# A network of attention, MLP and convolution on one core: LayerNorm multiplications placed elsewhere, two more taps for ScalarE, other banks and pace for the last image

## The chip, the cores and the metric

One core of a Trainium2 chip runs the whole program as one launch. The metric is device time in microseconds (us), the median of three runs. Engines are named as in the profile: PE is TensorE (matmuls), DVE is VectorE, ACT is ScalarE, POOL is GpSimd, SP is SyncE.

## The reference, cut to what matters

Eight images of 384 channels by 32 x 32 pixels, all in 32-bit floats. Each goes through a transformer block and then through a convolution block:

```python
# layer 0, tokens n = 1024 pixels, 8 heads of 48
xn = layernorm(x, g1, beta1);  q, k, v = xn @ w_qkv.T + b_qkv
x1 = softmax(q @ k.T * SCALE) @ v @ w_proj.T + b_proj + x
y  = x1 + gelu(layernorm(x1, g2, beta2) @ w_fc1.T + b_fc1) @ w_fc2.T + b_fc2   # hidden 1536
# layer 1
z = depthwise_conv_7x7(y) + dw_b
z = gelu(layernorm(z, ln_w, ln_b) @ w1 + b1)                                   # hidden 1536
gx = sqrt(sum over pixels of z*z);  nx = gx / (mean(gx) + eps)
out = y + (grn_gamma * (z * nx) + grn_beta + z) @ w2 + b2
```

The LayerNorms are called LN1 (ahead of q, k, v), LN2 (ahead of w_fc1) and LN3 (ahead of w1) below.

## The kernel before, in words

Channels lie on the 128 partitions, three tiles of them (CT = 3); pixels lie along the free axis, 1024 of them in two halves of 512. The images go through one after the other (main, L1611 on): the attention and the MLP of image b come first, then, inside the same pass of the loop, the second half of the convolution block of image b-1 (w1, GRN, w2), so that VectorE can convolve image b-1 while TensorE does the attention and the MLP of image b.

**Matmuls.** Attention is plain. fc1 is plain too, in halves of 512 tokens: gelu_half takes one ps_o bank, three matmuls and a Gelu on ScalarE (L457). fc2, w1, w2 and q/k use a fast scheme on 3 x 2 blocks with 15 products instead of 18, which needs sums of blocks. by_thirds (L919) does fc2 and w2: it forms sums of blocks of the hidden tensor, named f, h, e, g, by VectorE (L953) while the products run, and each product waits for its sum. tiles_by_thirds (L407) does w1 and q/k: here the block sums of the input are made ahead by make_thirds (L404) and VectorE adds up the outputs (L432) from single banks.

**PSUM.** Two pools: ps_s has two tiles of 128 x 1024 (attention's scores, every other product of fc2), ps_o has four tiles of 128 x 512 (everything else, the sums of the LayerNorms among them).

**Order.** The order of the instructions on each engine is that of the program, and the program is written out by a planner, Flow (L136). Flow.now is a clock that advances by U = 0.857 us with every full matmul that is written. A piece of side work is a Python generator (a chain); what it yields is the time until its next step is due, and a step is written once the clock has passed its due time. A paced chain counts from its due times, so that it catches up. finish(chain) writes all that is left of it at once.

**LayerNorm.** layernorm (L486) adds up the three tiles of channels on VectorE (L501, L503), has TensorE sum over the partitions with a matrix of ones (token_sums, L460), subtracts the mean (VectorE, L510), squares (ScalarE, L517), adds (L524), sums again, takes ln and exp on ScalarE (L534, L535) and multiplies (VectorE, L538). With fold, a GpSimd DMA first adds one half of the partitions onto the other (L475) and the ones matmul is half as large (L481); without, it is 128 x 128 (L467). abreast (L545) runs the two halves of an image as one chain, with all yields multiplied by factor (1.4).

- LN2 of the first half runs beside the end of attention (L810), spaced out and folded by "columns"; that of the second half runs beside fc1 of the first half (mlp, L893 on).
- LN3 of image b-1 (conv_norm, L1667) starts when LN2 of image b is through, after end_soon (L1700), which finishes the convolution's chains and then waits. It runs beside fc1's second half and fc2.
- LN1 of image b+1 (norm_of_next, L1704) runs beside the same stretch, with sums in places, four tiles of the pool tag "res". Its multiplications (L1757) come after a yield of 4.0, and are finished ahead of grn_up (the w1 matmuls).
- before_fc2 (L1760) finishes what is left of the convolution and spawns make_thirds for w1, after LN3.

**Convolution.** Of the 49 taps, convolution (L1072) writes 42 as VectorE instructions (L1098; the first L1096). The other seven (HELPED, L68) belong to help_convolution (L1103): for each tap and half of the image, ScalarE multiplies the window into a "res" tile (L1119), and a GpSimd DMA adds that onto the accumulator (L1120). It goes 2.7 us at a step, holds while `quiet` is set (the averages of attention, w2), and keeps VectorE off a tile of channels while it is at it (taken). For image 0, start_conv (L1661) is called behind its MLP; its convolution lies beside image 1's attention. The last image's convolution is written in two parts of its rows (last_convolution, L1783), each with its own pace; its LN3 goes in three parts of the pixels (LAST: 416, 288 and 320), and last_up (L1242) multiplies a part by w1 when its LN3 is finished.

**Image 0's preparations.** The sums of weight blocks and the products of weights with bias vectors are formed at the start, beside image 0, by the chains folds, prepare and sums_for_tiles. In shift_through_w2 (L1499), VectorE multiplies a third of w2 by grn_beta and adds it up (L1509 to L1511), and after a yield of 4.0 a matmul with ones takes the column sums (L273).

Of the kernel before, what the change touches and what calls it, by code (L numbers as in the profile page):

```python
# [46 lines left out]
F32 = mybir.dt.float32  # L47
# [4 lines left out]
P = 128  # L52
B, C, H, W = 8, 384, 32, 32
N = H * W
CT = C // P
# [120 lines left out]
def block_kernel(  # L176
# [280 lines left out]
        nc.scalar.activation(dst, src, function, **kw)  # L457
        table[0] = None

    def token_sums(t, name, fold, wait):  # L460

        width = t.shape[-1]
        if fold is None:
            total = o_tile(name)[:, :width]
            nc.tensor.matmul(out=total, lhsT=ones, rhs=t, start=True, stop=True)  # L467
            flow.pe(U * width / NH)
            return [(total, slice(0, width))]
        rows = [slice(0, 64), slice(64, P)]  # L470
        parts = [(fold, slice(0, width))]
        if fold == "columns":
            parts = [(j, slice(j * width // 2, (j + 1) * width // 2)) for j in range(2)]
        for j, cols in parts:
            nc.gpsimd.dma_start(out=t[rows[j], cols], in_=t[rows[1 - j], cols], accum_op=ALU.add)  # L475
        yield wait
        totals = []
        for j, cols in parts:
            total = o_tile(f"{name}_{j}")[:, : cols.stop - cols.start]
            for i in rows:  # L480
                nc.tensor.matmul(out=total[i, :], lhsT=ones[rows[j], :64], rhs=t[rows[j], cols], start=True, stop=True)  # L481
            flow.pe(U * width / NH / 2)
            totals.append((total, cols))
        return totals

    def layernorm(src, dst, h, eps, g, name, switch, spare=None, spaced=False, slow=1.0, fold=None, wait=3.4, gentle=False):  # L486

        cols = h if isinstance(h, slice) else half(h)
        if isinstance(h, slice):
            h = h.start
        width = cols.stop - cols.start
        if spare:
            a, *squares = (t[:, :width] for t in spare())
            rstd = a
        else:
            a = one.tile([P, NH], F32, tag="ln_a", name=f"{name}_a{h}")[:, :width]
        nc.vector.tensor_tensor(a, src[:, 0, cols], src[:, 1, cols], ALU.add)  # L500
        if gentle:  # L501
            yield 1.2
        nc.vector.tensor_tensor(a, a, src[:, 2, cols], ALU.add)  # L503
        yield 2.6 * slow
        totals = yield from token_sums(a, f"{name}_sum{h}", fold, wait)
        yield 0.8
        for ct in range(CT):
            for total, part in totals:
                to, of = dst[:, ct, cols][:, part], src[:, ct, cols][:, part]
                nc.vector.scalar_tensor_tensor(to, total, -1.0 / C, of, ALU.mult, ALU.add)  # L510
            if gentle:
                yield 1.2
        yield 0.8 * slow
        if not spare:
            squares = [three.tile([P, NH], F32, tag="ln_sq", name=f"{name}_sq{h}_{ct}")[:, :width] for ct in range(CT)]
        for ct in range(CT):
            nc.scalar.activation(squares[ct], dst[:, ct, cols], AF.Square)  # L517
            if spaced:
                yield 1.7
        yield 0.8 if spaced else 1.8 * slow  # L520
        nc.vector.tensor_tensor(squares[0], squares[0], squares[1], ALU.add)
        if gentle:
            yield 1.2
        nc.vector.tensor_tensor(squares[0], squares[0], squares[2], ALU.add)  # L524
        yield 1.8 * slow
        totals = yield from token_sums(squares[0], f"{name}_var{h}", fold, wait)
        yield 0.8

        if not spare:
            rstd = one.tile([P, NH], F32, tag="ln_rstd", name=f"{name}_rstd{h}")[:, :width]  # L530
        if switch:
            ln_table()
        for var, part in totals:
            nc.scalar.activation(rstd[:, part], var, AF.Ln, bias=eps, scale=1.0 / C)  # L534
        nc.scalar.activation(rstd, rstd, AF.Exp, scale=-0.5)  # L535
        yield (2.6 if switch else 1.2) * slow
        for ct in range(CT):
            nc.vector.scalar_tensor_tensor(dst[:, ct, cols], dst[:, ct, cols], col(g, ct), rstd, ALU.mult, ALU.mult)  # L538
            if gentle and ct < CT - 1:
                yield 1.2  # L540
# [1 line left out]
    def averages():  # L542
        return [attn[:, i, :] for i in range(4)]

    def abreast(*args, places=averages, fold=True, wait=3.4, gentle=False, factor=1.4):  # L545

        how = dict(wait=wait, gentle=gentle)
        chains = [
            layernorm(*args[:2], h, *args[2:], spare=places if h else None, fold=h if fold else None, **how)
            for h in range(2)  # L550
        ]
        while chains:
            waits = []
            for chain in list(chains):
                wait = next(chain, None)
                if wait is None:
                    chains.remove(chain)
                else:
                    waits.append(wait)
            if waits:  # L560
                yield factor * max(waits)
# [182 lines left out]
    def attention(b, xt, qT, kT, last_tile, ready, first, next_image):  # L744
# [44 lines left out]
        for n in range(len(steps) + 2):  # L789
            if n == 2:  # L790
                last_tile()
            if n < len(steps):
                if steps[n][0] == 0 and steps[n][2] == 0:
                    ready(steps[n][1])
                ps[n] = scores(*steps[n])
            if n >= 2:
                product(*steps[n - 2], ps.pop(n - 2))
            if n - 2 in (len(steps) // 2 - 9, len(steps) - 9):
                quiet.append("averages")
            if n - 2 == len(steps) // 2 + 6:  # L800
                for chain in first:
                    flow.finish(chain)
                xn = one.tile([P, CT, N], F32, tag="xn", bufs=2, name=f"xn2_{b}")
                next_image(b)
                for m in (NP - 1, *range(CT)):
                    flow.finish(chains[0, m])
                proj(b, xt, 0)
                quiet.clear()
                slow = 1.2 if b in (1, B - 1) else 1.0
                ln = layernorm(xt, xn, 0, eps0, "g2", f"ln2_{b}", False, spaced=True, slow=slow, fold="columns", wait=4.5)  # L810
                ln = flow.spawn(ln)

        def rest():
# [255 lines left out]
        rows, cols = inside(dy, dx, y0, y1)  # L1069
        return 120 + (rows.stop - rows.start) * (cols.stop - cols.start)  # L1070

    def convolution(acc, us, first=(), y0=0, y1=H, ready=tuple(range(CT)), taken=None):  # L1072

        done = [0] * CT
        ct, n = None, 0
        taps = KS * KS - (HELPED if taken is not None else 0)

        shares = [size(*divmod(i, KS), y0, y1) for i in TAPS[:taps]]  # L1080
        shares = [taps * s / sum(shares) for s in shares]
# [18 lines left out]
            n += 1  # L1100
            yield share * next((early for m, early in first if n <= m), us)

    def help_convolution(acc, us, taken):  # L1103

        yield 8.0
        for ct in reversed(range(CT)):
            taken[ct] = float("inf")
            for i in TAPS[KS * KS - HELPED :]:
                dy, dx = divmod(i, KS)
                for h in range(2):  # L1110
                    if quiet:
# [294 lines left out]
    def prepare(weights, aside):  # L1406
# [92 lines left out]
        def shift_through_w2():  # L1499
            for r in range(CT):  # L1500
# [8 lines left out]
                nc.vector.tensor_tensor(t[:, 0], t[:, 0], t[:, 1], ALU.add)  # L1509
                for k in range(1, h):  # L1510
                    nc.vector.tensor_tensor(t[:, 0, 0, :], t[:, 0, 0, :], t[:, 0, k, :], ALU.add)  # L1511
                yield 4.0
                ps = ps_s.tile([P, N], F32, tag="s", name=f"b2_{r}")
                column_sums(ps, 0, t[:, 0, 0, :])
                nc.vector.tensor_tensor(b2[:, r : r + 1], ps[:, :1], col("b2", r), ALU.add)
# [95 lines left out]
    def main():  # L1611
# [49 lines left out]
        def start_conv(b, us, *first):  # L1661
            acc = state["acc"] = one.tile([P, CT, N], F32, tag="acc", name=f"acc_{b}")
            taken = {}
            state["conv"] = flow.spawn(convolution(acc, us, first, taken=taken), paced=True)
            state["help"] = flow.spawn(help_convolution(acc, 2.7, taken), paced=True)

        def conv_norm(b, ln):  # L1667

# [3 lines left out]
                state["norm1"] = flow.spawn(after(ln, norm))  # L1672
            else:
                acc = state["acc"]
                how = dict(wait=5.0) if b < B - 1 else dict(wait=3.4, factor=2.4)
                norm = abreast(acc, acc, eps1, "lnw", f"ln3_{b - 1}", True, **how)
                if b < B - 1:
                    state["norm1"] = flow.spawn(after(ln, norm_of_next(b, 22.0 if b > 1 else 34.0)))
# [25 lines left out]
        def norm_of_next(b, us):  # L1704
# [8 lines left out]

            def total(t, h, kind):
                if kind == "sum":
                    ps = ps_s.tile([P, N], F32, tag="s", name=f"{name}_sum{h}")[:, :NH]
                else:
                    ps = o_tile(f"{name}_var{h}")
                for i in rows:
# [30 lines left out]
            for h, a, _ in pairs:  # L1750
                nc.scalar.activation(a, sums[h], AF.Ln, bias=eps0, scale=1.0 / C)
                nc.scalar.activation(a, a, AF.Exp, scale=-0.5)
            yield 4.0
            for h, a, _ in pairs:
                for ct in range(CT):
                    part = xn[:, ct, half(h)]
# [26 lines left out]
        def last_convolution(h, ct, ln=None):  # L1783
# [5 lines left out]
            ready[h].append(ct)  # L1789
            if ct == 0:  # L1790
                rows = (LAST[0].stop // W, H) if h else (0, LAST[0].stop // W)
                conv = convolution(last[0], 0.86 if h else 0.66, (), *rows, ready[h])
                state["conv"] = flow.spawn(after(state["conv"], conv), paced=True)
                if h == 0:
                    state["norm_a"] = flow.spawn(after(state["conv"], last_norm(LAST[0], 2.6)))

        for b in range(B):
# [29 lines left out]
            flow.finish(state["norm3"])  # L1827
            if b < B - 1:
                flow.finish(state["w1"])
                flow.finish(state["norm1"])  # L1830
                y, gx = grn_up(b - 1, weights, b - 1)
                start_conv(b, 1.6 if b == B - 2 else 1.65, (23, 2.4), (24, 9.0), (25, 26.0))
                scale = flow.spawn(grn_scale(b - 1, gx, weights, b - 1, y))
# [175 lines left out]
```

## Time and profile before

| what | us |
|---|---|
| median of three runs | 3280.41 (3280.2 to 3284.95) |
| profiled execution | 3279.71 |
| its span (1.8 lies around it) | 3277.9 |
| PE busy | 3239.4 (99%) |
| DVE busy | 2432.0 (74%) |
| ACT busy | 1662.0 (51%) |
| POOL busy | 480.3 (15%) |
| mean granted TensorE clock | 0.995 of full speed |

How to read it: the page gives busy times of each engine in one execution; a group of instructions is told by line, engine, operation and tile, out<-in. The waits of an engine list what its idle time ended with: "PE fc_p L445 <- ACT fc_n L943" is a matmul of line 445 into the tile fc_p that started when ScalarE's instruction of line 943 was done. A timeline gives start, duration, instruction and, in brackets, the idle time ahead of it with its releaser. A matmul of 128 x 512 has two records that overlap; start to start a full one takes 0.858 us. PEclk is the clock granted to TensorE. Where the work of the changed places lies, by the timeline: w2's shift at 100 to 160, LN2 of image 0 at 165 to 240, LN2 of image 1's second half until 531, fc2 and w1 of image 1 at 585 to 640, fc2 of image 3 at 1775 to 1800, LN3 of image 6 about 2950, and the last image's second part about 3150.

### The profile page before, as it was taken

The numbers are of one execution on the slowest core, as the hardware profiler recorded it, in microseconds if no ns is written. First come the engines' busy times: TensorE is split into PE (matmuls) and PEld (weight loads), VectorE is DVE, ScalarE is ACT, GpSimd is POOL, SyncE is SP. The second block draws the span as 40 slices with busy tenths as digits, with TensorE's granted clock in tenths as the row PEclk, the third lists the DMA queues.
The fourth block names the chain that finished last, engine by engine and source line by source line (L and its number), as shares of the span: only waits on it lengthen the run. The fifth ranks groups of instructions, "written<-read, shape, count | busy, mean of one in ns | idle before, by whom it ended". The sixth has DMA issues, their size and how long they took to land. (4 is left out here: it accounts for less than half of the span.)

```text
span 3277.9 us, 38879 instructions
## 1 busy us (share of the span) xinstructions
PE 3239.4 (99%) x14216; PEld 1399.7 (43%) x14216; DVE 2432.0 (74%) x3318; ACT 1662.0 (51%) x2317; POOL 480.3 (15%) x567
## 2 busy tenths in 40 slices
PE   9999999999999999999999999999999999999999
PEld 5344444343344433344344443444434443344455
DVE  4644788777877878768788687876888778879850
ACT  3442663356643475444753647537474365623631
POOL 2121211112110121101211012110221112200000
PEclk9999999999999999999999999999999999999999
DMA  6635742647335573446635375353843638433231
GB/s 213 221 100 121 165 87 57 156 108 172 82 65 154 120 161 75 87 138 153 139 64 115 110 189 100 63 128 103 204 91 67 157 91 189 73 79 85 68 91 54
DMA packets 202706, 384.82 MB, mean 117 GB/s; under 512 B 41104, under 2 KB 47120, under 8 KB 202128
## 3 DMA queue, kind: packets, MB, share of 16 engines
q0 software_dynamic: 81472, 166.50, 26.9%
q1 hardware_dynamic: 120752, 215.09, 21.5%
q8 instruction: 114, 1.87, 0.2%
q10 hardware_dynamic: 288, 0.71, 0.1%
q14 instruction: 80, 0.66, 0.1%
HBM read 199.61 MB, written 38.14 MB: 73 GB/s over the span
## 5 line engine op out<-in xcount | busy, mean ns | idle before, releaser
L1098 DVE SCALAR_TENSOR_TENSOR acc<-pad,vec,acc 128x870 f32<-128x870 f32 (+8 forms) x861 | 963.6, 1156 | 6.9 <-DMA acc<-tap 1.7
L764 ACT ACTIVATE p<-s 128x1024 f32<-128x1024 f32 x512 | 524.1, 1024 | 274.4 <-PE s L755 266.7
L755 PE MATMUL s<-qk 48*64 48x512 f32 x4096 | 549.5, 594 | 0.5 <-ACT qk L601 0.5
L775 PE MATMUL o<-p,v 64*64 64x512 f32 x4096 | 547.5, 593 | 0.0
L378 PE MATMUL fc<-xn,fc 128*128 128x512 f32 x1152 | 505.9, 596 | 2.1 <-DVE acc L510 2.1
L1120 POOL DMA_DIRECT2D acc<-tap x294 | 253.6, 872 | 1437.5 <-ACT tap L1119 704.2
L378 PEld LDWEIGHTS fc<-xn,fc 128*128 128x128 f32 x1152 | 217.7, 190 | 286.0 <-issue 275.6
L445 PE MATMUL fc_p<-hid,fc 128*128 128x512 f32 x728 | 319.7, 594 | 5.2 <-DVE hid L953 2.4
L775 PEld LDWEIGHTS o<-p,v 64*64 64x64 f32 x4096 | 168.1, 133 | 277.4 <-issue 269.0
L755 PEld LDWEIGHTS s<-qk 48*64 48x64 f32 x4096 | 163.4, 133 | 278.8 <-issue 223.8
L457 ACT ACTIVATE hid<-fc,bfc_f 128x512 f32<-128x512 f32 x192 | 129.9, 684 | 297.3 <-PE fc L378 297.2
L445 PE MATMUL o_p<-y,w 128*128 128x512 f32 x624 | 270.9, 592 | 0.0
L1119 ACT ACTIVATE tap<-pad,vec 128x512 f32<-128x512 f32 x294 | 215.8, 734 | 1.8 <-DMA acc<-tap 1.8
L445 PEld LDWEIGHTS fc_p<-hid,fc 128*128 128x128 f32 x728 | 137.0, 190 | 184.5 <-issue 169.4
L445 PEld LDWEIGHTS o_p<-y,w 128*128 128x128 f32 x624 | 118.0, 190 | 148.7 <-issue 134.9
L1098 DVE SCALAR_TENSOR_TENSOR acc_last<-pad,vec,acc_last 128x377 f32<-128x377 f32 (+24 forms) x288 | 177.3, 691 | 0.6
L887 ACT COPY pad<-x 128x512 f32<-128x512 f32 x48 | 30.2, 634 | 266.2 <-DVE x L953 209.2
L716 DVE TENSOR_TENSOR attn<-o,attn 128x512 f32<-128x512 f32 x64 | 44.1, 690 | 125.2 <-ACT attn L714 125.2
L697 PE MATMUL proj<-attn,wproj_sb 128*128 128x512 f32 x288 | 127.5, 596 | 0.7 <-DVE attn L742 0.7
L675 PE MATMUL v<-wv_sb,xn 128*128 128x384 f32 x384 | 126.8, 487 | 0.0
L432 DVE TENSOR_TENSOR y<-h_n,y 128x512 f32<-128x512 f32 x72 | 49.8, 692 | 74.6 <-PE h_n L416 72.2
L675 PEld LDWEIGHTS v<-wv_sb,xn 128*128 128x128 f32 x384 | 72.5, 190 | 50.1 <-issue 3.3
(376 smaller groups left out, 4068.3 us busy)
## 6 DMA issues: line engine op xcount, KB each, us to landing
acc<-tap POOLq DMA_DIRECT2D x294, 256.0 KB, 3.5
fc<-s_fc SPq DMA_DIRECT2D x91, 256.0 KB, 3.0
w<-s_w SPq DMA_DIRECT2D x72, 320.0 KB, 3.1
hid<-hid POOLq DMA_DIRECT2D x42, 512.0 KB, 7.1
fc<-in_wfc SPq DMA_DIRECT2D x54, 384.0 KB, 4.0
w<-s_w SPq DMA_DIRECT2D x78, 256.0 KB, 2.7
y<-y POOLq DMA_DIRECT2D x36, 512.0 KB, 6.8
w_A<-in_w SPq DMA_DIRECT2D x36, 384.0 KB, 3.2
```

What stands on the lines that cost most here:

```text
L378: nc.tensor.matmul(out=ps, lhsT=lhsT(k), rhs=rhs(k)[:, half(h)], start=(k == 0), stop=(k == nk - 1))
L432: nc.vector.tensor_tensor(c[dst], banks(name), c[other], ALU.add)
L445: nc.tensor.matmul(out=bank, lhsT=lhsT, rhs=rhs, start=k == 0, stop=k == len(pairs) - 1)
L457: nc.scalar.activation(dst, src, function, **kw)
L675: nc.tensor.matmul(out=ps[:, :C], lhsT=xn[:, k, t * P : (t + 1) * P], rhs=wv_sb[:, k, :], start=(k == 0), stop=(k == CT - 1),)
L697: nc.tensor.matmul(out=ps, lhsT=wproj_sb[:, m, ct * P : (ct + 1) * P], rhs=attn[:, m, :], start=(m == 0), stop=(m == CT - 1),)
L755: nc.tensor.matmul(out=s[64 * i : 64 * i + 64, j, :], lhsT=kT[64 * j : 64 * j + HD, m, k0 : k0 + 64], rhs=qT[64 * j : 64 * j + HD, m, half ...
L764: nc.scalar.activation(p, s, AF.Exp)
L775: nc.tensor.matmul(out=outs[i][64 * j : 64 * j + 64, :], lhsT=v[keys, t, at : at + 64], rhs=p[keys, j, :], start=(t == 0), stop=(t == KT - 1),
L1098: nc.vector.scalar_tensor_tensor(dst, window, tap, dst, ALU.mult, ALU.add)
L1119: nc.scalar.mul(t.rearrange("p (h w) -> p h w", w=W), window, tap)
L1120: nc.gpsimd.dma_start(out=acc[:, ct, half(h)], in_=t, accum_op=ALU.add)
```

## The change

1. s_tile gives a ps_s tile; token_sums, layernorm and abreast take `bank`, from which the sums' tile comes. For the last pass (LN3 of image 6), bank is s_tile.
2. layernorm takes `late`, added to the yield ahead of its multiplications. LN3 of the other images has late=3.5 (4.9 after the factor).
3. norm_of_next yields 50.0 instead of 4.0 ahead of its multiplications, and is no longer finished ahead of grn_up; it is finished by next_values, behind grn_up.
4. LN2 of image 0's first half isn't folded.
5. ScalarE has nine taps instead of seven for image 0 (convolution and help_convolution take `helped`).
6. shift_through_w2 yields 8.0 instead of 4.0 ahead of its matmul (three times).
7. The second part of the last convolution has a pace of 0.76 us instead of 0.86 per tap.

```diff
+    def s_tile(name):
+        return ps_s.tile([P, N], F32, tag="s", name=name)
+
-    def token_sums(t, name, fold, wait):
+    def token_sums(t, name, fold, wait, bank):
...
-            total = o_tile(f"{name}_{j}")[:, : cols.stop - cols.start]
+            total = bank(f"{name}_{j}")[:, : cols.stop - cols.start]
...
-    def layernorm(src, dst, h, eps, g, name, switch, spare=None, spaced=False, slow=1.0, fold=None, wait=3.4, gentle=False):
+    def layernorm(src, dst, h, eps, g, name, switch, spare=None, spaced=False, slow=1.0, fold=None, wait=3.4, gentle=False, bank=o_tile, late=0):
...
-        yield (2.6 if switch else 1.2) * slow
+        yield (2.6 if switch else 1.2) * slow + late
...
-                ln = layernorm(xt, xn, 0, eps0, "g2", f"ln2_{b}", False, spaced=True, slow=slow, fold="columns", wait=4.5)
+                fold = "columns" if b else None
+                ln = layernorm(xt, xn, 0, eps0, "g2", f"ln2_{b}", False, spaced=True, slow=slow, fold=fold, wait=4.5)
...
-        taps = KS * KS - (HELPED if taken is not None else 0)
+        taps = KS * KS - helped
...
-            for i in TAPS[KS * KS - HELPED :]:
+            for i in TAPS[KS * KS - helped :]:
...
-                yield 4.0
+                yield 8.0
                 ps = ps_s.tile([P, N], F32, tag="s", name=f"b2_{r}")
...
-            state["conv"] = flow.spawn(convolution(acc, us, first, taken=taken), paced=True)
-            state["help"] = flow.spawn(help_convolution(acc, 2.7, taken), paced=True)
+            helped = HELPED if b else HELPED + 2
+            state["conv"] = flow.spawn(convolution(acc, us, first, taken=taken, helped=helped), paced=True)
+            state["help"] = flow.spawn(help_convolution(acc, 2.7, taken, helped), paced=True)
...
-                how = dict(wait=5.0) if b < B - 1 else dict(wait=3.4, factor=2.4)
+                how = dict(wait=5.0, late=3.5) if b < B - 1 else dict(factor=2.4, bank=s_tile)
...
-            yield 4.0
+            yield 50.0
             for h, a, _ in pairs:
                 for ct in range(CT):
                     part = xn[:, ct, half(h)]
...
-                conv = convolution(last[0], 0.86 if h else 0.66, (), *rows, ready[h])
+                conv = convolution(last[0], 0.76 if h else 0.66, (), *rows, ready[h])
...
                 flow.finish(state["w1"])
-                flow.finish(state["norm1"])
                 y, gx = grn_up(b - 1, weights, b - 1)
```

## The prediction

> **What bounds the kernel now.** I read the busy times first, then TensorE's waits over the run, then the timeline and the windows around each wait that the change touches.
>
> ```profile
> span 3277.9 us, 38879 instructions
> PE 3239.4 (99%) x14216; PEld 1399.7 (43%) x14216; DVE 2432.0 (74%) x3318; ACT 1662.0 (51%) x2317; POOL 480.3 (15%) x567
> ```
>
> TensorE is busy for 99% of the span and idle for 38.5 us. No matmul of weight goes away, so all that can be won is in these waits and in slow matmuls behind them:
>
> ```profile
> PE fc_p L445 <- ACT fc_n L943: 5.6, 5, 1.1
> PE b L273 <- DVE w_gbeta L1511: 3.0, 1, 3.0
> PE h_n L416 <- ACT y L437: 2.5, 1, 2.5
> PE ln_var L467 <- DVE ln_sq L524: 2.4, 1, 2.4
> PE fc_p L445 <- DVE hid L953: 2.4, 6, 0.6
> PE fc L378 <- DVE acc L510: 2.1, 1, 2.1
> PE ln_sum L481 <- DMA ln_a<-ln_a: 2.0, 1, 2.0
> PE fc_p L445 <- DVE fc_e L953: 2.0, 5, 0.4
> PE h_last L1250 <- DVE acc_last L538: 1.6, 1, 1.6
> ```
>
> (Columns: sum, count, longest.) The fc_p rows come once per image in fc2; the others once each. VectorE just ahead of such a wait, image 3, and TensorE behind it:
>
> ```profile
> 1781.10 0.75 DVE L1757 SCALAR_TENSOR_TENSOR xn<-xn,vec,ln 128x512 f32<-128x512 f32 x1
> 1784.16 0.74 DVE L1757 SCALAR_TENSOR_TENSOR xn<-xn,vec,ln 128x512 f32<-128x512 f32 x1
> 1784.82 1.22 DVE L953 TENSOR_TENSOR fc_e<-hid 128x1024 f32<-128x1024 f32 x1
> ```
>
> ```profile
> 1783.03 1.98 PE L445 MATMUL fc_p<-hid,fc 128*128 128x512 f32 x4 [0.37 <-DVE hid L953]
> 1786.14 1.96 PE L445 MATMUL fc_p<-fc_e,fc 128*128 128x512 f32 x4 [1.12 <-ACT fc_n L943]
> 1788.49 1.98 PE L445 MATMUL fc_p<-fc_e,fc 128*128 128x512 f32 x4 [0.40 <-DVE fc_e L953]
> ```
>
> The LayerNorm multiplications (L1757 here, L538 at 1777 to 1781) stand between the additions that make fc2's block sums; 1786.14 is when fc_e of 1784.82 is done. Windows (us, PE busy, clock, DMA, GB/s) show what a long wait costs besides:
>
> ```profile
> 120.00:124.00 4.00, 4.00 (x28) 0.57 0.71 233
> 3158.80:3162.20 3.40, 2.56 (x5) 0.50 0.00 0
> ```
>
> **What the Trainium skill says.** "TensorE: Matmul & The Clock Gate", "What's actually happening": the clock falls to half after an idle window of about 3.4 us and returns after a busy one. The trace agrees on the half rate, 0.57 after the 3.01 us wait and 0.50 after the 2.45 us one, but there a shorter idle stretch was enough; 1.12 us was not. I count 1.6 us beside a wait of over 2 us. Same page, "Architectural detail: the array is 16× 32×32, not 1× 128×128": VectorE's and ScalarE's queues are strict FIFO; the order above agrees. "DMA: Bandwidth & Descriptors", "Rules for kernel authors": an accumulating DMA must wait for an earlier one on the same bytes; GpSimd waited 54 times, 139.6 us, for acc<-tap.
>
> **The change part by part** (minus is time won; a 128x512 matmul is 0.858 us start to start).
>
> *fc2's multiplications, images 2 to 6.* Before each fc2 they cost 0.53 + 1.39 + 0.63 + 0.10 = 2.65 us beyond 0.858 us per matmul, start to start. LN3's six multiplications go 4.9 us later (3.5 x 1.4), behind the first block sum; LN1's six leave fc2 for w1's matmuls (grn_up): 12 x 0.66 us leave the chain, more than its lateness. No DMA is in the moved steps. Won 5 x 2.65 = 13.2. In grn_up each of the six lies ahead of VectorE's block adds; a bank returns after three matmuls, which leaves some 0.68 us for one 0.66 us multiplication: I take 0.2 us per image, bounds 0 and 6 x 0.67 = 4.0. Sum **-12.2**.
>
> *Image 1's fc2 and w1.* The same, and the 2.5 us wait for y (L437). Losses 0.64 + 0.66 + 2.6 + 4.25 = 8.2 start to start; the first two stay (1.3), of the last some 1.7 wait and 0.8 clock stay, 0.6 is added by LN1 in grn_up, 0.2 by rounding: **-3.6** (-2 to -5.5).
>
> *The shift's yield 8.0, image 0.* The matmul at 119.37 waits 3.01 us for a VectorE step that ends at 119.23. 4 us later, it finds it done: 3.0 + 1.6 + 0.1: **-4.7**. What queues behind, attention's matmuls, is ready.
>
> *LN2 of image 0 without the fold.* Gone: two GpSimd DMAs and the matmul's 2.03 us wait at 171.16; from 168.08 to 175.05 the work takes 3.8 us over its nominal time. Added: two full ones matmuls, 0.86 instead of 0.58 us each, 0.56; and as the sums come 4.5 us sooner, the third w_gbeta product (4.4 us of VectorE) lies ahead of LN2's subtractions, ScalarE's squares wait for these and the exponentials behind them: 0.85. **-2.4** (0 to -3.3).
>
> *LN3 of image 6 on ps_s banks.* Sums held in two of the four ps_o banks keep fc1 (L378) waiting for VectorE: 2.07 us, and 36 records take 17.32 us instead of 15.43. Attention is over, its ps_s banks are free ("PSUM — Partial Sum Buffer", "Specifications (TRN2)": eight banks; here 4 + 2 x 2, as the shapes show). **-4.1**.
>
> *The last taps' pace 0.76.* 147 taps x 0.10 = 14.7 us earlier. VectorE has room: it idles 3.72, 1.09, 1.29, 1.52 and 1.00 us ahead of the output additions (L1214) of 3111 to 3152. So the taps' lateness is their pace. The second part's LN3 is then nearly done before its matmuls; its last multiplications still go out behind the fifth addition of 3152.41, 1.2 us. The waits 1.70 + 2.45 + 1.62 + 0.7 and 2.8 of clock make 9.3 now: **-8.1**.
>
> *Two more taps by ScalarE, image 0.* VectorE loses six taps of 1.16 us, which TensorE does not wait for. ScalarE and GpSimd gain 12 half-taps:
>
> ```profile
> L1119 ACT ACTIVATE tap<-pad,vec 128x512 f32<-128x512 f32 x294 | 215.8, 734 | 1.8 <-DMA acc<-tap 1.8
> DMA to landing us min/median/max: 3.2/3.5/9.2
> 522.83 0.72 ACT L1119 ACTIVATE tap<-pad,vec 128x512 f32<-128x512 f32 x1
> ```
>
> The 42 half-taps of before end at 522.83, because the helper holds during attention and goes 2.7 us each after. LN2's second half ends about 531; end_soon (L1700) then flushes what is left. Three more get out in 531 - 523, nine do not: they are written at once into ScalarE's queue, ahead of fc1's gelus. LN1's sums hold two of the four "res" buffers, so the taps share two, and each waits for the landing of the tap two before: a pair takes 0.73 + 0.3 + 3.55 = 4.6 us, behind the two folds of 532.69. ScalarE is free about 552.5, the first gelu ends at 553.3. TensorE fills its four banks until 541.7, then waits 11.6 us, and 1.7 of clock: **+13.3** (0 to 19; 0 if more of them get out earlier). VectorE's flushed taps wait for the last landing (556.7), end by 574, and LN3's sums are needed at 585.7: nothing further.
>
> Sum: -12.2 - 3.6 - 4.7 - 2.4 - 4.1 - 8.1 + 13.3 = -21.8. From the profiled execution's 3279.71 this gives 3257.9; the median of the runs is 0.7 above it: **3258.6**.
>
> **The rivals.** (1) The flush is covered: the taps get out in attention's gaps, or land beside the gelus. Then -35.1: **3245**. For it: the helper's pace is counted in matmuls, and my count of three is exact only if that clock runs as I worked it out; against it: 42 end just 8 us before the flush. (2) Multiplications in grn_up hold the banks: each of the 36 costs 0.67 us, 24 instead of the 1.6 counted: **3281**, the same as before. Against it: they come one every second matmul. (3) Slower: the flushed accumulates land at the pace of the worst one seen, 9.2 us. Nine taps on two buffers make about four rounds; without the flush -35.1 us is won, so with a landing of (35.1 + 0.8)/4, about 9.0 us, all is lost; beyond, at 10 to 11 us with clock, **3284 to 3290**. Against it: the median is 3.5 us. (4) LN3 of the last image doesn't get earlier, since VectorE is full there (111.6 us of work in 112): half of the 8.1 is lost, **3263**.
>
> **How the numbers follow.** Forecast 3258.6, with rival 4's shade, 0.66; rival 1 0.22; rival 2 0.07; rival 3 0.04; 0.01 for what I haven't thought of. A measurement here can tell about 0.2%, 6.6 us, from no change. Rivals 2 and 3 are left outside the range (0.11), so it goes from rival 1 less 3 us, 3242, to the forecast with the flush at 19 us and half of the last part lost, 3270. Faster by over 0.2%: 0.66 + 0.22 + a little = 0.90; same 0.06; slower 0.04.
>
> **What would show it.** Right: the fc_n, hid and fc_e rows gone from images 2 to 6 and L1757 among w1's matmuls; no wait at 119 and 171; fc L378 not waiting for acc L510; h_last's waits under 2 us in all; one wait of some 12 us of fc in image 1's second fc1 half, released by ScalarE's gelu, with L1119 queued ahead. Wrong: no such wait (3245), or h_n waiting for VectorE's y in every image (3281).

## The result and the profile after

The changed kernel takes 3272.17 us (median of nine runs) against 3282.91 us for the kernel before (nine runs beside them); the ratio is 0.9969, with a 95% interval of 0.9958 to 0.9979. It is faster by 10.7 us. The forecast was 3258.6, within 3242 to 3270, so the measured time lies outside the range by 2.2 us: the direction held, half of the gain did not come. The profiled execution took 3271.23 us.

The head of the page after, to lay beside the one of before:

```profile
span 3269.3 us, 38881 instructions
PE 3231.1 (99%) x14204; PEld 1396.2 (43%) x14204; DVE 2423.7 (74%) x3309; ACT 1670.5 (51%) x2328; POOL 487.1 (15%) x575
```

Two instructions more in all, DVE with nine fewer, ACT and POOL with more. TensorE's waits after (sum, count, longest):

```profile
PE fc L378 <- ACT hid L457: 15.3, 1, 15.3
PE s L758 <- DVE b_f L1519: 5.6, 1, 5.6
PE fc L378 <- DVE x L895: 2.2, 1, 2.2
PE fc_p L445 <- DMA hid<-hid: 2.0, 1, 2.0
PE h_n L416 <- ACT y L437: 1.8, 1, 1.8
PE h_last L1254 <- DVE acc_last L541: 1.3, 1, 1.3
PE b L273 <- ACT p L767: 1.2, 1, 1.2
```

(The lines after are up to 5 higher than before: L755 is now L758, L1098 is L1102, L1515 is L1519.) The fc_n, hid and fc_e rows of fc2 are gone but for image 1's. Four rows name waits that before did not have at all: the two long ones at the top, the third and the last.

To place the time I took the k-th matmul of each tile in both traces and subtracted the start before from the start after. This difference is called the lead below: plus means that the changed kernel is behind at that matmul, minus that it is ahead. A stage's own part is how much the lead changes in it, the matmuls at half clock included:

| stretch (us of before) | lead from, to | forecast | measured |
|---|---|---|---|
| 0 to 168: shift through w2 | 0, +3.1 | -4.7 | +3.1 |
| 168 to 240: LN2 of image 0 | +3.1, -0.2 | -2.4 | -3.2 |
| 240 to 530: before the flush | -0.2, -1.8 | 0 | -1.7 |
| 530 to 560: flush, image 1's fc1 | -1.8, +16.8 | +13.3 | +18.6 |
| 590 to 640: image 1's fc2, w1 | +16.8, +13.6 | -3.6 | -3.2 |
| fc2 of images 2 to 6 | five steps of -2.66 | -12.2 | -13.3 |
| 640 to 2940, all else | | 0 | -0.4 |
| 2948 to 2960: LN3 of image 6 | -0.2, -1.6 | -4.1 | -1.5 |
| 3060 to 3200: last taps | -1.6, -8.7 | -8.1 | -7.0 |

The flush in the trace after. (The flush is what end_soon writes at once of the convolution that is left; a half-tap is one tap on one half of the image.) ScalarE, its last two half-taps and the gelus behind them:

```profile
550.98 0.74 ACT L1123 ACTIVATE tap<-pad,vec 128x512 f32<-128x512 f32 x1 [0.86 <-DMA acc<-tap]
553.78 0.74 ACT L1123 ACTIVATE tap<-pad,vec 128x512 f32<-128x512 f32 x1 [2.06 <-DMA acc<-tap]
554.42 2.40 ACT L457 ACTIVATE hid<-fc,bfc_f 128x512 f32<-128x512 f32 x4
```

and TensorE, which filled its four banks until 539.9 and went on when the first gelu was through:

```profile
525.13 14.75 PE L378 MATMUL fc<-xn,fc 128*128 128x512 f32 x34
555.14 29.06 PE L378 MATMUL fc<-xn,fc 128*128 128x512 f32 x60 [15.26 <-ACT hid L457]
```

The shift through w2. Some of VectorE's steps between the matmul of 118.52 and the addition that gives back its bank, then TensorE's scores:

```profile
119.83 1.22 DVE L1376 TENSOR_TENSOR qk<-qk 128x128 f32<-128x128 f32 x5
121.24 2.12 DVE L1376 TENSOR_TENSOR qk<-qk 128x128 f32<-128x128 f32 x7
123.47 0.68 DVE L719 TENSOR_TENSOR attn<-o,attn 128x512 f32<-128x512 f32 x1
124.66 0.69 DVE L745 TENSOR_TENSOR attn<-attn,r 128x512 f32<-128x512 f32 x1
125.27 0.15 DVE L1519 TENSOR_TENSOR b_f<-b,vec 128x1 f32<-128x1 f32 x1
```

```profile
118.52 0.35 PE L273 MATMUL b<-ones,w_gbeta 128*128 128x1 f32 x2 [1.19 <-ACT p L767]
125.48 1.98 PE L758 MATMUL s<-qk 48*64 48x512 f32 x8 [5.59 <-DVE b_f L1519]
```

The matmul no longer waits for its sums. But its one column lies in a ps_s tile, one of the two that the scores alternate in, and the addition that frees the tile is now written behind 24 small steps on weights and two steps of the averages. Before, it was done at 122.24.

The gain, fc2 of image 3: TensorE goes through from 1777.71 without a wait, and LN1's multiplications lie among w1's additions:

```profile
1781.25 10.46 PE L445 MATMUL fc_p<-hid,fc 128*128 128x512 f32 x24
1791.55 3.60 PE L445 MATMUL fc_p<-fc_e,fc 128*128 128x512 f32 x8
```

```profile
1827.80 0.74 DVE L1762 SCALAR_TENSOR_TENSOR xn<-xn,vec,ln 128x512 f32<-128x512 f32 x1
1828.87 0.69 DVE L432 TENSOR_TENSOR y<-h_n,y 128x512 f32<-128x512 f32 x1 [0.33 <-PE h_n L416]
```

### The profile page after: what moved, and what is told of

Same layout as the page of the kernel before. It is cut to its first block, busy times and chain, and to the rows that moved or that the text cites. A ratio compares the mean times of both kernels' runs of the same rounds, so it can differ in the third digit from the quotient of the medians.

```text
span 3269.3 us, 38881 instructions
## 1 busy us (share of the span) xinstructions
PE 3231.1 (99%) x14204; PEld 1396.2 (43%) x14204; DVE 2423.7 (74%) x3309; ACT 1670.5 (51%) x2328; POOL 487.1 (15%) x575
## 5 line engine op out<-in xcount | busy, mean ns | idle before, releaser
L1102 DVE SCALAR_TENSOR_TENSOR acc<-pad,vec,acc 128x930 f32<-128x930 f32 (+8 forms) x855 | 956.9, 1156 | 29.2 <-DMA acc<-tap 24.4
L758 PE MATMUL s<-qk 48*64 48x512 f32 x4096 | 539.9, 594 | 5.8 <-DVE b_f L1519 5.6
L778 PE MATMUL o<-p,v 64*64 64x512 f32 x4096 | 536.4, 591 | 0.0
L378 PE MATMUL fc<-xn,fc 128*128 128x512 f32 x1152 | 507.6, 597 | 17.4 <-ACT hid L457 15.3
L1124 POOL DMA_DIRECT2D acc<-tap x306 | 263.4, 874 | 1449.1 <-ACT tap L1123 727.7
L758 PEld LDWEIGHTS s<-qk 48*64 48x64 f32 x4096 | 159.4, 133 | 285.8 <-issue 221.4
L1123 ACT ACTIVATE tap<-pad,vec 128x512 f32<-128x512 f32 x306 | 224.6, 734 | 19.6 <-DMA acc<-tap 19.6
L1102 DVE SCALAR_TENSOR_TENSOR acc_last<-pad,vec,acc_last 128x377 f32<-128x377 f32 (+24 forms) x288 | 177.2, 690 | 0.6
```

Of the source, the lines that this page charges most:

```text
L378: nc.tensor.matmul(out=ps, lhsT=lhsT(k), rhs=rhs(k)[:, half(h)], start=(k == 0), stop=(k == nk - 1))
L758: nc.tensor.matmul(out=s[64 * i : 64 * i + 64, j, :], lhsT=kT[64 * j : 64 * j + HD, m, k0 : k0 + 64], rhs=qT[64 * j : 64 * j + HD, m, half ...
L778: nc.tensor.matmul(out=outs[i][64 * j : 64 * j + 64, :], lhsT=v[keys, t, at : at + 64], rhs=p[keys, j, :], start=(t == 0), stop=(t == KT - 1),
L1102: nc.vector.scalar_tensor_tensor(dst, window, tap, dst, ALU.mult, ALU.add)
L1123: nc.scalar.mul(t.rearrange("p (h w) -> p h w", w=W), window, tap)
L1124: nc.gpsimd.dma_start(out=acc[:, ct, half(h)], in_=t, accum_op=ALU.add)
```

## The experiments

All are edits of the changed kernel; e1 to e16 are the runs in their order. Times are medians; a ratio is to the kernel before, run on the same chip. Not all experiments ran on the chip of the changed kernel's own runs, so two experiments are compared by their ratios or by the leads, not by their medians. A lead in this part is taken against the changed kernel, unless the text says otherwise.

**The flush (e1 to e4).** The edit is the number of taps for image 0, or the helper's pace:

```diff
-            helped = HELPED if b else HELPED + 2
+            helped = HELPED                        # e1; + 1 in e2, + 3 in e3
...
-            ... help_convolution(acc, 2.7, taken, helped) ...
+            ... help_convolution(acc, 2.7 if b else 2.2, taken, helped) ...   # e4
```

> The changed kernel with part 5 undone: seven taps by ScalarE for image 0 as for the others. Theory (flush): fc1's one wait of 15.3 us for ScalarE's gelu is gone with the nine half-taps that end_soon writes ahead of it, and the half clock behind it, so the time falls by about 18 us against the changed kernel, to about 3254; image 1's fc2 keeps its 2.0 us wait for the DMA of hid only if that came from the late LN3, so up to 1.5 us more may go. Rival (VectorE): the six taps that VectorE gets back (6.9 us) fall into the same stretch and hold LN1's and LN3's additions as long as the flush did; then less than half of it, 0 to 8 us, is won, and a wait for VectorE stands at the same place.

3254.49 us, 0.9913 (0.9899 to 0.9926). No wait of fc1 is left; the lead goes from +1.4 to -17.2 us in that stretch. The rival is out: with VectorE's six taps back, no wait for VectorE stands in the place of the flush.

> The changed kernel with one more tap by ScalarE for image 0 instead of two: 48 half-taps, of which 45 get out before the flush, so three are left instead of nine. Theory (flush, set by the number of half-taps that are left, each pair at 4.4 us): the third one starts at about 540.6 as in the changed kernel, TensorE resumes about 1.4 us behind it, at 542 instead of 555, a wait of some 2 us, with at most 1 us of clock: 3 us slower than with seven taps, 14 to 15 us faster than with nine, about 3257. Rival (the flush costs by being there, because the folds and the landings hold ScalarE whatever the number): a wait of over 8 us stays, and the time is above 3263.

3254.24 us, 0.9912 (0.9896 to 0.9927). The wait is 2.1 us, as expected; by the leads it is 2.6 us behind e1, which the times don't tell:

```profile
PE fc L378 <- ACT hid L457: 2.1, 1, 2.1
```

> The changed kernel with three more taps by ScalarE for image 0 instead of two: 60 half-taps, 15 left at the flush. Theory (flush): six more half-taps on two buffers are three more pairs of 4.4 us, so the wait of fc1 for the gelu grows from 15.3 to about 28.4 us and the time by 13 us against the changed kernel, to about 3285. Rival (VectorE is what ends the stretch, and it has three taps less): the wait stays below 20 us, and the time within 5 us of the changed kernel's.

3283.77 us, 1.0 (0.9992 to 1.0009): with three more taps instead of two, all that the change wins is given back.

```profile
PE fc L378 <- ACT hid L457: 27.0, 1, 27.0
```

With 0, 3, 9 and 15 half-taps left at the flush the wait is 0, 2.1, 15.3 and 27.0 us: from three on, some 2 us for each half-tap, half of a pair's 4.4.

> The changed kernel with nine taps, but image 0's helper goes at 2.2 us a half-tap instead of 2.7. The two stretches in which it may go are about 120 us together, so 20% more of them fit: all 54 are out before LN2's second half ends. Theory (flush): no half-tap is left for the flush, fc1's wait goes, and the time is that of the kernel with seven taps, about 3254, less nothing, since TensorE doesn't wait for the six taps of VectorE. Rival (the accumulations need their 3.5 us of landing and GpSimd's queue falls behind, or ScalarE's exponentials are held by the denser taps): waits of attention's matmuls for ScalarE's p appear, and the time is 3260 or more.

3259.11 us, 0.9928 (0.9912 to 0.9943). All 54 half-taps are out and fc1 doesn't wait, so it isn't the number of taps but what is left of them that costs. The rival has a share: image 1's first scores and q/k wait 2.3 us for ScalarE (0.6, 1.1 and 0.6), where the denser taps lie.

**The shift and LN2 of image 0 (e5, e6, e12, e7).**

```diff
-                yield 8.0
-                ps = ps_s.tile([P, N], F32, tag="s", name=f"b2_{r}")
+                yield 4.0                          # e5 only
+                ps = o_tile(f"b2_{r}")             # e6 and e12
...
-                yield 14.0
+                yield 14.0 if r == 0 else 10.0     # e12
...
-                fold = "columns" if b else None
+                fold = "columns"                   # e7
```

> The changed kernel with part 6 undone: the shift through w2 yields 4.0 ahead of its matmul again. Theory (release): with 8.0 the matmul no longer waits for its sums, but the ps_s tile it takes is given back only by VectorE's one-column addition, which is queued behind more small weight additions, and the scores wait 5.6 us for that tile, with 1.7 us of half clock. Undone, that wait is gone and the 3.0 us wait of before with its 1.6 us is back: 4 to 6 us faster than the changed kernel, about 3267. Rival (the lost time belongs to LN2 without the fold, which moves the same chain): the 5.6 us wait stays and the time is within 2 us of the changed kernel's, or slower by 3 to 5 us, as part 6 was to win 4.7.

3269.03 us, 0.9963 (0.9949 to 0.9977). The median is 3 us lower, but the intervals of the two ratios overlap. By the leads e5 is ahead of the changed kernel by 1.8 us at 158 and by 1.5 at 240, less than half of what was expected; what it wins further on lies for the most part in image 1, at a wait for a DMA that varies from run to run whatever the edit (see e9). The wait that came back is 5.4 us and not 3.0:

```profile
118.62 0.56 PE L273 MATMUL b<-ones,w_gbeta 128*128 128x1 f32 x2 [5.39 <-DVE w_gbeta L1515]
```

TensorE came 3.1 us earlier than before (at full clock, see the last section), and VectorE was done only 0.7 us earlier, at 118.5 instead of 119.2.

> The changed kernel, yield 8.0 kept, but the shift's matmul writes to a ps_o bank instead of a ps_s tile. Theory (release): the scores no longer need the tile that VectorE is late to give back, so the waits of 5.6 us (scores for the addition) and 1.2 us (the matmul for the exponential that holds the tile) go with their clock: 8 us faster than the changed kernel, about 3264. Rival (any bank is short there): attention's outputs need two of the four ps_o banks per pair of heads and two are held by the averages, so a wait of 4 to 6 us appears at the outputs (L778) instead, and the gain is under 3 us.

3272.68 us, 0.9968 (0.9956 to 0.9981): no gain. The scores' wait is gone, as the theory had it, so the tile was the cause of it; the gain is under 3 us, as the rival had it, but the wait in its place is not at attention's outputs. The projection waits, and the matmul at 121 waits 1.6 us for its sums. VectorE and TensorE in e6:

```profile
143.43 1.82 DVE L1512 TENSOR_TENSOR w_gbeta<-w_gbeta,vec 128x768 f32<-128x768 f32 x2
148.59 0.19 DVE L726 RECIPROCAL inv<-sums 128x8 f32<-128x8 f32 x1
155.40 0.69 DVE L745 TENSOR_TENSOR attn<-attn,r 128x512 f32<-128x512 f32 x1 [2.07 <-DMA r<-back]
```

```profile
156.15 7.97 PE L700 MATMUL proj<-attn,wproj_sb 128*128 128x512 f32 x14 [3.69 <-DVE attn L745]
```

The longer yield also moves the next product of the chain, 4.4 us of VectorE, ahead of the reciprocal that the averages need. That calls for putting it back:

> The changed kernel with two edits in the shift through w2: its matmul writes to a ps_o bank, and the yield ahead of the second and third product is 10.0 instead of 14.0, so that these come where they were before. Theory: with the bank alone the scores' wait of 5.6 us was gone and the output projection then waited 3.7 us for the averages, because the second product (4.4 us of VectorE) stood ahead of the reciprocal of the averages; with the product at its old place, that wait is back under 1 us: 5 to 6 us faster than the changed kernel, about 3267. Rival (the averages' own DMAs end there whatever stands on VectorE): the projection's wait stays at 3 us or more, and the time within 2 us of the changed kernel's.

3268.47 us, 0.9958 (0.9941 to 0.9975). The median is near what was expected, but that doesn't bear the theory out: by the leads e12 is 1.0 us behind the changed kernel at 240, and what it is ahead at the end comes later. The projection doesn't wait any more, but the product now stands ahead of another addition that frees a tile:

```profile
138.58 1.59 DVE L1515 TENSOR_TENSOR w_gbeta<-w_gbeta 128x128 f32<-128x128 f32 x5
140.09 0.15 DVE L1501 TENSOR_TENSOR b_f<-b,vec 128x3 f32<-128x3 f32 x1
```

```profile
140.30 1.44 PE L273 MATMUL b<-ones,w_lnb 128*128 128x1 f32 x6 [5.00 <-DVE b_f L1501]
```

So the wait stood at four places in five kernels (3.0 and 5.4 for the sums, 5.6 for the scores, 3.7 for the projection, 5.0 here). Each time TensorE waited for VectorE, and no order tried here is without a wait. VectorE isn't simply full: in the changed kernel it stands idle for 4.51 us, until 112.38, for the DMA of the sums that the averages need, and the product for w2 is queued behind that step. What an earlier DMA would be worth was not tried.

> The changed kernel with part 4 undone: LN2 of image 0's first half is folded by GpSimd again. Theory: the wait for the fold's DMA (2.0 us at 171) and the matmuls at half clock behind it come back, some 3 us slower than the changed kernel, about 3275. Rival (the fold's wait was there only because the preparations ahead of it were where they were, and is now covered since they run later): within 1 us of the changed kernel.

3272.42 us, 0.9971 (0.9963 to 0.998): the rival is right. With part 6 in, part 4 is worth nothing that can be told. GpSimd before (first fence) and in e7 (second):

```profile
163.00 3.19 POOL L1425 DMA_DIRECT2D w_a<-in_w  x6 [4.69 <-PE b L273]
166.18 1.75 POOL L475 DMA_DIRECT2D ln_a<-ln_a  x2
```

```profile
165.55 1.71 POOL L478 DMA_DIRECT2D ln_a<-ln_a  x2 [3.10 <-DVE ln_a L506]
177.24 3.28 POOL L1429 DMA_DIRECT2D w_a<-in_w  x6 [9.98 <-PE b L273]
```

Before, the fold was queued behind six loads of weights; the longer yields alone move these behind it. In e5, without the longer yields, part 4 is worth 2.4 us by the leads of e5 against the kernel before (from +0.8 at 158 to -1.6 at 240).

**fc2 (e9, e10, e13).**

```diff
-                how = dict(wait=5.0, late=3.5) if b < B - 1 else ...
+                how = dict(wait=5.0) if b < B - 1 else ...           # e9 and e13
...
-            yield 50.0
+            yield 4.0                                                # e10 and e13
...
+                flow.finish(state["norm1"])                          # e10 and e13, ahead of grn_up
```

> The changed kernel with the late=3.5 of part 2 undone: LN3's six multiplications stand between fc2's first sums again, LN1's six stay in w1's matmuls. Theory (a chain with slack): VectorE's sums in fc2 have some 3.4 us of slack in the changed kernel (the sums of fc_e end at 1787.9, their product starts at 1791.55), and six multiplications take 4.0 us, so only 0.5 to 1 us per image comes back, 3 to 5 us in all for images 2 to 6, about 3276. Rival (each half of the move is worth its half): 1.3 us per image, 6.6 us in all, about 3279. Rival (LN3's place alone made the waits): all of the 2.65 us per image, 13 us, about 3285.

3270.45 us, 0.9964 (0.9955 to 0.9973). Not one us comes back in images 2 to 6: the lead stays at -0.9 from 700 to 2700. Image 1 is 1.5 us better, as its wait for the DMA of hid is 0.5 instead of 2.0 us. That isn't the lateness: e5, e10, e12 and e14 have it and wait 0.4 to 0.5 us, e13 and e15 don't have it and wait 2.0. What goes with the wait is the time from that DMA's issue to its landing: 9.8 to 9.9 us in the runs where the wait is 2.0, 8.4 to 8.7 in those where it is 0.6 or less. Why one transfer has two landing times stays open.

> The changed kernel with part 3 undone: LN1's six multiplications come after a yield of 4.0 in fc2 again and are finished ahead of the w1 matmuls; LN3's stay late. Theory (a chain with slack): as in the run with late undone, 4.0 us of multiplications against some 3.4 us of slack, but they are spread over the sums, so 0.5 to 1 us per image, 3 to 5 us in all, about 3276; the multiplications that lay among w1's block additions cost nothing there, so nothing is won for taking them away. Rivals as there: 6.6 us (half of the move), or 13 us (LN1's place alone made the waits).

3275.93 us, 0.9981 (0.9974 to 0.9987). The larger loss, 4.7 us, lies in image 1's w1 (h_n waits 3.7 instead of 1.8); images 2 to 6 lose 0.8 us in all, and all of that in image 3.

> The changed kernel with parts 2 and 3 both undone: LN3's and LN1's multiplications are all in fc2 again. Theory (a chain with slack for six, not for twelve): undone one at a time, either cost nothing in images 2 to 6; together they exceed the slack and all of the 2.65 us per image is back, 13 us for five images, with image 1's waits some 16 us in all, about 3286. Rival (another part of the change took these waits away): less than 5 us slower than the changed kernel.

3289.93 us, 1.0022 (1.0015 to 1.0029; of its twenty executions one took 13130.55 us, which the median doesn't feel). Fc2's waits are back to the tenth:

```profile
PE fc_p L445 <- ACT fc_n L947: 5.6, 5, 1.1
PE fc_p L445 <- DVE hid L957: 2.4, 6, 0.6
PE fc_p L445 <- DVE fc_e L957: 2.0, 5, 0.4
```

The lead grows by 2.66 us at each of the five fc2, so 13.3 us of the change's gain are shown to be those of parts 2 and 3, where either alone is nearly enough: there was slack for six multiplications and not for twelve. Six take 4.0 us and cost nothing or 0.8, so the slack was larger than the 3.4 us that I read off.

**The last image (e8, e11, e14).**

```diff
-                conv = convolution(last[0], 0.76 if h else 0.66, ...
+                conv = convolution(last[0], 0.86 if h else 0.66, ...           # e8
...
-                ... else dict(factor=2.4, bank=s_tile)
+                ... else dict(factor=2.4)                                      # e11
+                ... else dict(wait=8.0, factor=2.4, bank=s_tile)               # e14
```

> The changed kernel with part 7 undone: the last convolution's second part at 0.86 us per tap again. Theory (pace): the LN3 of the second part comes 14 us later again, its three waits of 1.7, 2.5 and 1.6 us and the half clock return: 7 to 8 us slower than the changed kernel, about 3280. Rival (VectorE is full there, the pace decides little): under 4 us slower.

3277.7 us, 0.9987 (0.998 to 0.9994); by the leads 7.0 us slower at that place. The waits of 1.7, 2.4 and 1.6 us are back.

> The changed kernel with part 1 undone for the last image: LN3 of image 6 sums in ps_o banks again. Theory (the wait was replaced): fc1's wait of 2.1 us for LN3's subtraction (L513) with its half clock returns, and the wait of 2.2 us for fc2's addition (L895), which queues behind the same subtractions on VectorE, goes: 1.5 us slower than the changed kernel by the place of the matmuls behind it, at the edge of what the times can tell, 3272 to 3275. Rival (the two waits are independent): both are there, and it is 4 us slower, about 3276.

3270.87 us, 0.996 (0.9946 to 0.9974), not to be told from the changed kernel by the times; by the leads 1.4 us slower at that place. The wait for L513 is back with 2.0 us, that for L895 gone: one takes the other's place. The 1.4 us are half clock, which e11 has behind its wait and the changed kernel's trace hasn't. Six other runs with the changed kernel's code at this place (e1, e6 to e9 and e13) have the same wait for L895 and lose 1.5 to 1.6 us by half clock behind it; seven (e2 to e5, e10, e12 and e15) lose nothing. So part 1 isn't shown to win anything.

> The changed kernel, but LN3 of image 6 waits 8.0 instead of 3.4 (times 2.4) ahead of its sums, so that they come 11 us later and VectorE's six subtractions lie behind fc2's addition. Theory: the wait of 2.2 us for that addition (L895) at 2955 goes, no other takes its place, since w1 needs LN3 only at 3010 and it would be done by about 2996: 2.2 to 2.6 us faster by the place of the matmuls behind it, about 3269.5. Rival (VectorE is late there through the taps alone): the wait stays at 1.5 us or more. Rival (LN3 comes too late for w1): a wait at 3010 in its place.

3272.35 us, 0.9967 (0.9954 to 0.998). The wait at 2955 went, and 2.54 us were won there, as expected. At 3080 they were lost again and 3.2 us more, at a place that neither theory named: the wait is 2.6 us, and the clock granted from 3082 to 3088.8 was 0.51 and 0.50 in its two halves:

```profile
3082.68 7.53 PE L1254 MATMUL h_last<-acc_last,w_A 128*128 128x416 f32 x12 [2.62 <-DVE gmean L1271]
```

The mean of image 6's GRN is on VectorE behind a row of 30 taps that begins at 3060.9, and came at 3082.5, in the changed kernel at 3082.2: TensorE is earlier, VectorE isn't.

**Together (e15, e16).** e15 has the edits of e1, e5 and e9; e16 that of e14 too.

> The changed kernel with three losing parts undone: seven taps by ScalarE for image 0, the shift's yield 4.0, LN3's multiplications not late; kept are LN1 in w1's matmuls, LN2 of image 0 without the fold, LN3 of image 6 in ps_s, the pace 0.76. Theory (the losses add up): 17.7 us for the flush, 2 to 3 for the shift, 1.3 for image 1's fc2, so 21 to 22 us faster than the changed kernel, about 3250. Rival (they overlap, since a wait that goes lets the next one show): not faster than the kernel with seven taps, 3254.

3252.38 us, 0.9908 (0.9895 to 0.9922), the lowest median here, but within the interval of e1. The flush alone is worth most of it. The yield of 4.0 adds 2.1 us by the leads of e15 against e1 at 240, though the wait for the sums is 6.0 us; undoing the lateness adds nothing, as image 1's wait for the DMA of hid is 2.0 us again. Whether the losses add up, the times can't tell.

> The kernel with three parts undone, and LN3 of image 6 later as in the run e14_sums_later. Theory: its 2.2 to 2.6 us are independent of the rest, so about 3247.5, the fastest of all here. Rival: no difference to the kernel with three parts undone.

3253.81 us, 0.9915 (0.9901 to 0.9928): the rival, no difference in the times; the wait for gmean is there with 2.6 us as in e14, this time at full clock.

## Why the prediction was wrong

By its own steps, largest miss first; with the two rows of the table that were forecast as 0, the misses add up to 13.2 us, which is the shortfall in the profiled execution.

- *"What queues behind, attention's matmuls, is ready"* (the shift, -4.7; +3.1 by the leads, a miss of 7.8). This step failed. I asked whether the matmul's operand would be done, and not which tile it takes and who gives that back. The Trainium skill ("TensorE: Matmul & The Clock Gate", "Architectural detail: the array is 16× 32×32, not 1× 128×128") was cited for VectorE's strict first-in-first-out queue, and I did not apply the same rule to the addition behind the matmul; the trace agrees with it, as the scores wait 5.59 us for that addition. At 158 us, ahead of LN2, the lead is +2.6 with the yield of 8.0 and +0.8 in e5, which has the old one, so part 6 itself costs 1.8 us there (1.5 at 240) where I had it win 4.7. The 3.3 us that the clock had given both of them by 110 (last section) were lost again: they wait for VectorE in any case.
- *The flush, +13.3*: the mechanism was right in every step (three half-taps get out, nine are left, two buffers, the four banks filled until 539.9), and e1 to e3 show it. Two terms were mis-sized. One is when the pairs start: VectorE came to LN1's sums later, so the folds were issued at 535.19, where I had 532.69 less the 1.8 us by which TensorE led, and the wait was 15.3 instead of 11.6 us. The other is the half clock behind it: seven matmuls took 0.85 to 1.01 us start to start instead of 0.43, 3.1 us where I had 1.7. Together 18.6 by the starts. As a pair took 4.4 us, the landings were not slow: rival 3 is out.
- *LN3 of image 6, -4.1* (its two terms, 2.07 and 1.89, make 4.0), got 1.5. I removed the wait and did not ask what is next: fc2's addition (L895) was behind the same six subtractions (e11), and the wait for it is 2.18 us. What was won is the half clock, which this execution doesn't have there and others do; e14 shows a third wait behind that.
- *The pace, -8.1*: 7.0, with e8, so rival 4 (half of it lost) is out.
- *Image 1, -3.6*: 3.2; its wait for the DMA of hid grew from 0.5 to 2.0 us, as the DMA landed 1.5 us later (e9), so without that it would have been more than forecast.
- *Images 2 to 6, -12.2*: 13.3, as in each image 2.66 us went, and the multiplications among w1's additions cost nothing where I counted 1.0; rival 2 is out.
- *LN2 without the fold, -2.4*: right by itself (2.4 in e5; in the leads 2.7 from 158 on, 3.2 from 168 on), but the fold's wait would have gone through part 6 as well (e7), so the two were not to be added.
- Rival 1, the flush covered, was given 0.22 and would be e1's 3254; it is not what happened. The range ended at 3270, with a flush of 19 us and half of the last part lost; it had no bound for the shift ending as a loss, though a wait in place of the one removed was the case to allow for.
- The half clock was priced at 1.6 us beside any wait of over 2 us. In these traces it is 0 or 1.5 to 1.6 us behind the same wait of 2.2, and 0 or 3.2 behind the same wait of 2.6 (e16, e14). So where a part matches its forecast to a few tenths, that may be luck.

Not tried: what the flush costs with four buffers to itself.

## What to carry to other kernels

When a step is moved, list what it holds until it is through (a bank, a tile, a place in a queue) and follow who releases that: the wait that goes is often one of several deadlines on the same engine, and the next one stands a few us behind it. Work that is flushed ahead of a deadline costs little while little is left of it (here 2.1 us with three half-taps left) and its length from there on (some 2 us for each further one): count what is left. A gain that two edits share can't be added up: undo each alone and both together. And before a difference of 1 or 2 us at one place is called an edit's work, look at the same place in runs whose edits lie elsewhere.

## What the runs showed of the hardware

TensorE's clock isn't the same in each execution at the same place. The lines are those of before and after, behind the same wait of a quarter us for the one-column matmuls at 101:

```profile
103.31 1.89 PE L775 MATMUL o<-p,v 64*64 64x512 f32 x8
104.97 1.93 PE L755 MATMUL s<-qk 48*64 48x512 f32 x8
```

```profile
101.67 1.04 PE L778 MATMUL o<-p,v 64*64 64x512 f32 x8
102.53 1.04 PE L758 MATMUL s<-qk 48*64 48x512 f32 x8
```

Granted were 0.52 in one and 1.00 in the other, 1.7 us for nothing that the program does; the stretch at 70 us has 1.6. The Trainium skill ("TensorE: Matmul & The Clock Gate", "What's actually happening") fits in part: by it the window in which activity is watched runs freely, so the number of slow matmuls differs from run to run. But it puts the fall of the clock down to an idle window of about 3.4 us, and the wait here is 0.26 us, behind twelve one-column matmuls. What brought the clock down stays open. Over the sixteen experiments the lead at 112 us, behind this stretch, lies between 0 and +5.6.

The same holds behind a wait. The changed kernel and e7 wait 2.18 us for fc2's addition at 2955 and 2957; the windows (us, PE busy, clock, DMA, GB/s) behind it:

```profile
2955.00:2958.40 3.40, 3.35 (x8) 1.00 0.00 0
2957.20:2960.60 3.40, 3.35 (x5) 0.60 0.00 0
```

What the clock gives is lost again where VectorE sets the pace (e5), and stays where nothing waits (behind 2955 it is there to the end). The times don't tell two of these kernels apart by less than some 3 us; the leads do place by place, but 1.5 us in one trace can be the clock alone.
